# Third and fourth token block share up_w and fc1_w, by seven half-size products; the second block's last product becomes the plain one

## The chip, the cores and the metric

The kernel runs on one core of a Trainium2 chip. Its time is in device microseconds (us); the time before is the median of three runs. A profile is one execution, with the engines named PE (matrix products), PEld (their weight loads), DVE (vector engine), ACT (scalar engine), POOL (GpSimd) and SP (which issues most transfers).

## The reference

One decoder layer over x of 2 x 512 tokens with 1024 features, all f32. What is computed, cut to what matters:

```python
def _L0_attn_ref(x, Wq, bq, Wk, bk, Wv, bv):          # attention inside each token
    q = jnp.einsum('bse,edh->bsdh', x, Wq) + bq         # 32 x 32
    ...                                                 # k, v: 32 x 8, repeated 4 times
    scores = jnp.einsum('bsdh,bseh->bsde', q, k) / np.float32(np.sqrt(D))
    attn = jax.nn.softmax(scores, axis=-1)
    out = jnp.einsum('bsde,bseh->bsdh', attn, v)
def _L0_xattn_ref(x1, x2, ...):                         # per batch
    return jnp.matmul(fake_quant(x1, ...), fake_quant(x2, ...))
def _L0_ffn_ref(hidden_states, gate_w, up_w, down_w, fc1_w, fc2_w, expert_w, ln_gamma, ln_beta):
    logits = jnp.einsum('bsh,he->bse', hidden_states, gate_w)
    routing_weights, selected_experts = jax.lax.top_k(logits, K)
    h = jax.nn.relu(jnp.einsum('bsh,hi->bsi', hidden_states, up_w)) ** 2
    shared_out = jnp.einsum('bsi,ih->bsh', h, down_w)
    x_latent = jnp.einsum('bsh,hl->bsl', hidden_states, fc1_w)
    expert_out = jnp.einsum('bsl,lm->bsm', x_latent, expert_w)
    moe_out = expert_out * jnp.sum(routing_weights, axis=-1, keepdims=True)
    routed_out = jnp.einsum('bsl,lh->bsh', moe_out, fc2_w)
    return _layernorm(shared_out + routed_out, ln_gamma, ln_beta)
x = _layernorm(x + attention(x)); x = _layernorm(x + xattn(x, ctx)); x = _layernorm(x + ffn(x))
```

up_w is 1024 x 2048, down_w 2048 x 1024, fc1_w 1024 x 512, and expert_w x fc2_w (called e2) is 512 x 1024.

## The kernel before

The 1024 tokens are eight tiles of 128, and two tiles make a block of 256; there are four blocks (0 and 1 of batch 0, 2 and 3 of batch 1). Each engine runs its own instructions in the order in which they were laid out, and waits at an instruction whose operand isn't there.

*Front (to 153 us).* `load_xT`, `project_qk` (L148) and `project_v` project all tiles; `fill` lays out side work, the quantised context of batch 0 and e2 (L417). Queries, keys and values of tiles 2 to 7 go to DRAM and are fetched back on POOL's queue.

*Token path.* `token_path` takes the tiles one after another. Attention is on DVE: `scores` (L433, L439), `exponentials`, `attend` (L464, L470, and L485, which adds the result to the row). Then ACT normalises the row aside (`normalise_aside`, with a power on POOL at L323), and `cross` quantises it on ACT (up to L590), transposes it by a DMA on ACT's queue (L593) and multiplies it with the quantised context on PE (py, L607). Another normalisation follows, and `hand_over` transposes the row on PE (L129) into x2T and adds beta to the row by an accumulating DMA from an SBUF tile. `context_beside` makes the context of batch 1 while block 0 and 1 are in work; `context_row` sums its columns on PE (pc, L548).

*Block loop.* For each block, `ffn` does the gate (L708), then 16 products of up_w and 4 of fc1_w (L745: eight matmuls of 128x128 by 128x256 each), with relu (L772) and square (L773) on ACT, and the product with the routing rows on DVE (L786). The weights are loaded by SP, 1 MB for two products, into two buffers (wstream). Each block loads all of them for itself. Between the products the driver at the end of the kernel lets the token path of the next block move on, paced by `PACE`; PE's order is therefore a mix of products, crossings and transposes.

*Down product.* Block 0 uses `down`: 20 units of 128 rows (16 of down_w, 4 of e2), each times two token tiles and two halves of the output (L866, 128x512). Blocks 1 to 3 use `down_seven` (`BY_SEVEN = 1`): a product of 2 x 2 sub-blocks by seven products of half size in place of eight. It needs sums of the units (`unit_sums`, L893 to L896), sums of the weights (`weight_sums`, L906 to L908), both on DVE, seven products (L952, 128x256) in the order 1, 6, 7, 5, 4, 2, 3, and combinations of their results on ACT and DVE (L963 to L972). `finish` normalises, scales and adds the residual row; for blocks 0 to 2 the last normalisation is put aside on ACT (`store_aside`), for block 3 it is done at once at the end.

*Buffers.* Four buffers hold token rows (xpool). PSUM has eight banks: four in ps_dn, two in ps_mm, two in ps_tr.

Of the kernel before, what the change touches and what calls it, by code (L numbers as in the profile page):

```python
# [9 lines left out]
F32 = mybir.dt.float32  # L10
# [17 lines left out]
def kernel(  # L28
# [45 lines left out]
    PACE = (0.9, 0.8, 0.8, 0.8)  # L74
    GW = 32
    NK = NI + NL
    BY_SEVEN = 1
# [7 lines left out]
    xpool = ctx.enter_context(tc.tile_pool(name="xc", bufs=4))  # L85
# [8 lines left out]
    ps_dn = ctx.enter_context(tc.tile_pool(name="ps_dn", bufs=4, space=PSUM))  # L94
    front = ExitStack()
# [5 lines left out]
    identb = const.tile([P, P], BF16, name="identb")  # L101
# [14 lines left out]
    bqk = const.tile([P, 2 * DG], F32, name="bqk")  # L116
    bv_ge = const.tile([P, G, D], F32, name="bv_ge")
# [45 lines left out]
    def new_qkv(t, away):  # L163
        bufs = KEPT if away else 2
        qk = attp.tile([P, 2 * DG], F32, tag="s12" if away else "qk", name=f"qk_{t}", bufs=bufs)
        v = attp.tile([P, G, D], F32, tag="s4" if away else "v", name=f"v_{t}", bufs=bufs)
        return qk, v
# [30 lines left out]
    brow = attp.tile([P, E], F32, tag="s", name="brow", bufs=2)  # L198
    bqk_row = attp.tile([P, E], F32, tag="s", name="bqk_row", bufs=2)
# [6 lines left out]
    ones_row = const.tile([P, P], F32, name="ones_row")  # L206
# [77 lines left out]
    beta = const.tile([P, E], F32, name="beta")  # L284
# [80 lines left out]
    def fill():  # L365
# [3 lines left out]
        for t in range(TB, NT):  # L369
            for _ in range(2):  # L370
                next(aside, None)
            if t == NT - 3:
                nc.sync.dma_start(gamma, ln_gamma.partition_broadcast(P))
                nc.sync.dma_start(beta, ln_beta.partition_broadcast(P))
            ps = projection_psum(t)
            following = None
            for k in range(KE):
                project_qk(ps[0], xT, k)
                project_v(ps[1], xT, k)
                if k == 3:  # L380
                    yield 5.2
                if k == 4 and t + 1 < NT:

                    following = load_xT(t + 1)
                    lay_bias(t + 1)
                    yield 1.3
            xT = following
            projected(t, *ps)
            yield 5.2
# [15 lines left out]
        for l in range(NL):  # L405

            while l >= NL // 2 and 1 not in crossed:
                yield 1.0
            if l == NL // 2:
                with tc.issue_after(expert[0].ins):  # L410
                    held.pop()()
            row = work.tile([P, E], F32, tag="work", name=f"e2_{l}")
            for n in range(2):
                ps = ps_mm.tile([P, HALF], F32, tag="mm", name=f"pe2_{l}_{n}")
                with tc.issue_after(crossed[1].ins) if l >= NL // 2 else ExitStack():
                    for m in range(NL):
                        expert[0] = nc.tensor.matmul(  # L417
                            ps, exT[:, m, ts(l, P)], fc2[m // 2][:, m % 2, ts(n, HALF)],
                            start=(m == 0), stop=(m == NL - 1),
                        )  # L420
                nc.scalar.copy(row[:, ts(n, HALF)], ps)
                yield 3.5
            nc.gpsimd.dma_start(e2[ts(l, P), :], row)


    def scores(t, qk, behind=None):
        q3 = qk[:, 0:DG].rearrange("p (d g) -> p d g", g=G)
        k3 = qk[:, DG : 2 * DG].rearrange("p (e g) -> p e g", g=G)
        s = attp.tile([P, D, D], F32, tag="s", name=f"s_{t}", bufs=2)
        for c in range(D // DC):  # L430
            prod = attp.tile([P, DC * D * G], F32, tag="prod", name=f"pqk_{t}_{c}", bufs=2)
# [22 lines left out]
    def attend(t, xc, s, v):  # L454
# [6 lines left out]
        o = attp.tile([P, D, G], F32, tag="o", name=f"o_{t}")  # L461
        for c in range(D // DC):
            prod = attp.tile([P, DC * D * G], F32, tag="prod", name=f"pav_{t}_{c}", bufs=2)
# [30 lines left out]
    def context_tiles(b):  # L494

        cq = cqs[b] = const.tile([P, KC, E], BF16, tag="cq", name=f"cq_{b}")
# [9 lines left out]
    def context_beside(b):  # L506
# [20 lines left out]
        cq = cqs[b] = const.tile([P, KC, E], BF16, tag="cq", name=f"cq_{b}")  # L527
# [13 lines left out]
    def context_row(b, cq):  # L541
        crow = const.tile([P, E], F32, tag="crow", name=f"crow_{b}")
        for h in range(E // HALF):
            pc = ps_mm.tile([P, HALF], F32, tag="mm", name=f"pc_{b}_{h}")

            with tc.issue_after(projecting[0].ins):
                for k in range(KC):
                    nc.tensor.matmul(  # L548
                        pc, onesb, cq[:, k, ts(h, HALF)], start=(k == 0), stop=(k == KC - 1)
                    )  # L550
# [7 lines left out]
    crossed, held, lately, up_to = {}, [], [None], [0]  # L558
# [6 lines left out]
    def cross(t, xc, cq, crow):  # L565
# [3 lines left out]
        aT = attp.tile([P, KC, P], BF16, tag="aT", name=f"aT_{t}")  # L569
# [29 lines left out]
        for h in range(E // HALF):  # L599

            if t < TB or up_to[0] >= t // TB:
                py = ps_mm.tile([P, HALF], F32, tag="mm", name=f"py_{t}_{h}")
            else:
                py = ps_dn.tile([P, HALF], F32, tag="dn", name=f"py_{t}_{h}")
# [19 lines left out]
    def token_path():  # L624
# [3 lines left out]
        for blk in range(NBLK):  # L628
            xcs = []
            x2T = []  # L630
            for i in range(TB):
# [35 lines left out]
                def hand_over(blk=blk, t=t, i=i, xc=xc, x2T=x2T):  # L667
                    if not x2T:
                        x2T.append(attp.tile([P, KE, NB], F32, tag="x2T", name=f"x2T_{blk}"))
# [3 lines left out]
                    nc.gpsimd.dma_start(xc, beta, accum_op=ALU.add)  # L673
# [3 lines left out]
                if t == 0 or up_to[0] < blk:  # L677
                    held.append(hand_over)
# [20 lines left out]
    def ffn(blk, xcs, xT):  # L699
        (xT,) = xT  # L700
        t0 = blk * TB
        xcs_of[blk] = xcs
# [9 lines left out]
        lg = small.tile([P, NB], F32, tag="lg", name=f"lg_{blk}", bufs=1)  # L712
        nc.scalar.copy(lg, pg[:, :NB])
        yield 1.5


        rwb = pools["ffn"].tile([P, NB], F32, tag="rwb", name=f"rwb_{blk}")

        rwms = []

        def routing():
            for i in range(TB):
                pl = ps_tr.tile([P, NE], F32, tag="tr", name=f"plg_{t0 + i}")
                nc.tensor.matmul(pl, lg[:, ts(i, P)], sel, start=True, stop=True)
                top = small.tile([P, 8], F32, tag="top", name=f"top_{t0 + i}")
                nc.vector.max(top, pl)
                rw = small.tile([P, 1], F32, tag="rw", name=f"rw_{t0 + i}")
                nc.vector.tensor_add(rw, top[:, 0:1], top[:, 1:2])
                rwm = small.tile([P, P], F32, tag="rwm", name=f"rwm_{t0 + i}", bufs=2)
                nc.vector.tensor_copy(rwm, rw.to_broadcast([P, P]))  # L730
                rwms.append(rwm)

        def routing_rows():

            for i, rwm in enumerate(rwms):
                pw = ps_tr.tile([P, P], F32, tag="tr", name=f"pw_{t0 + i}")
                with tc.issue_after(lately[0].ins):
                    nc.tensor.transpose(pw, rwm, ident)
                nc.scalar.copy(rwb[:, ts(i, P)], pw)
# [10 lines left out]

        h, sums = [], []

        def piece(k):
            if k % 4 == 0:
                h.append(pools["h"].tile([P, TB, 4, P], F32, tag="h", name=f"h_{blk}_{k // 4}"))
            return h[-1][:, :, k % 4, :]

        def halves(t):
            return t.rearrange("p (i n) -> p i n", n=P)

        def sums_due():

            while blk >= BY_SEVEN and len(sums) < len(h) - 1:
                sums.append(unit_sums(blk, len(sums), h[len(sums)]))

        for c in range(INT // CW):
# [9 lines left out]
            sums_due()  # L776
            if c == 1:
                routing()
            if c == INT // CW - 2:
                routing_rows()  # L780
        for c in range(LAT // CW):
# [6 lines left out]
            sums_due()  # L788

        up_to[0] = blk + 1  # L790
        if (blk + 2) * TB == S // P:
            later.append(context_beside(1))
        while held:
            held.pop(0)()
        if blk < BY_SEVEN:
            yield from down(blk, h)
        else:
            sums.append(unit_sums(blk, len(sums), h[-1]))
            yield from down_seven(blk, h, sums)
# [16 lines left out]
    def finish(blk, i, y, parts, stats=None):  # L816
# [8 lines left out]
        if blk < NBLK - 1:  # L825
# [6 lines left out]
        nc.vector.scalar_tensor_tensor(y, y, rstd, xcs_of[blk][i], ALU.mult, ALU.add)  # L832

# [21 lines left out]
    def down(blk, h):  # L855
# [4 lines left out]
        for c in range(NK // 2):  # L860
            w = down_rows(f"dn_{blk}_{c}", 2 * c, 2, 0, E)
            for k in range(2):
# [7 lines left out]
                beside(1)  # L870
# [40 lines left out]
    def down_seven(blk, h, units):  # L911
# [17 lines left out]
        while g < len(groups):  # L929
# [27 lines left out]
            yield 6.1 * along  # L957
# [24 lines left out]
    def block_of(step):  # L982
        return step if isinstance(step, tuple) else None

    ready, w_tok, w_fill = None, 0.0, 0.0
    while ready is None:
        step = next(tokens)
        ready = block_of(step)
        w_tok += 0.0 if ready else step
# [15 lines left out]
    for blk in range(NBLK):  # L1005
        now, ready = ready, None
        w_tok = w_ffn = 0.0
        for weight in ffn(*now):
            w_ffn += weight
            while blk + 1 < NBLK and ready is None and w_tok * PACE[blk] < w_ffn:  # L1010
                step = next(tokens)
                ready = block_of(step)
                w_tok += 0.0 if ready else step
        while blk + 1 < NBLK and ready is None:
            ready = block_of(next(tokens))
# [33 lines left out]
```

## Time and profile before

| | us |
|---|---|
| median of three runs (733.94 to 737.42) | 736.36 |
| profiled execution | 740.23 |
| its span | 738.5 |
| PE starts block 0, 1, 2, 3 (gate) | 152.69, 302.62, 451.75, 592.40 |
| PE ends the last product | 724.92 |
| L745, all up_w and fc1_w products, PE busy | 226.4 + 55.9 |
| L866, plain down of block 0 | 69.2 |
| L952, down by sevens of blocks 1, 2, 3, four groups | 61.0 + 61.0 + 60.9 + 30.5 |

| stretch, us | PE busy | DVE busy | ACT busy | granted clock |
|---|---|---|---|---|
| 153 to 303 | 148.70 | 143.50 | 54.54 | 1.00 |
| 303 to 450 | 143.69 | 132.51 | 60.00 | 0.99 |
| 450 to 592 | 141.60 | 70.86 | 44.34 | 1.00 |
| 592 to 740 | 132.07 | 56.38 | 22.39 | 0.96 |

A line of the groups reads: line, engine, operation, output<-inputs, shapes, count, busy time, mean ns of one, and the idle time just before them with what ended it. The granted clock is the share of full speed that the throttle left to PE. Matmuls overlap, so that the mean ns of one is longer than the distance from one to the next.

### The profile page before, as it was taken

Reading aid. Unit: us, or ns where it says so; the run is one execution under the profiler, and the core shown is the slowest. Engines: PE = TensorE matmul, PEld = TensorE weight load, DVE = VectorE, ACT = ScalarE, POOL = GpSimd, SP = SyncE. Lnnn points to the kernel's source line nnn. Section 1 sums busy time; section 2 is a strip of 40 time slices with the busy share of each in tenths; the row PEclk is TensorE's granted clock in tenths of the full one; section 3 lists DMA queues with packets and bytes.
Section 4 is the critical chain, followed back from the end, with each engine's and each line's share of the span. In section 5 each row is a group of like instructions: output and inputs, shape, how many; then the busy total and the mean of one; then the engine's idle time right before and its main releaser. Section 6 shows DMA issues by size and latency. Waiting matters only on the chain. (4 is left out here: it accounts for less than half of the span.)

```text
span 738.5 us, 7687 instructions
## 1 busy us (share of the span) xinstructions
PE 708.4 (96%) x3002; PEld 533.7 (72%) x3012; DVE 523.5 (71%) x573; ACT 248.7 (34%) x433; POOL 69.2 (9%) x96
## 2 busy tenths in 40 slices
PE   6999998999999999998999999999999999999992
PEld 3665653468876444686788788887887888888882
DVE  4789986699989999999999968913246371013636
ACT  2087633222573205377560021374401013400001
POOL 2001221100001002130010011010000010100001
PEclk9999998999999999999999999999999999999997
DMA  8999635294546547764456446564654645635401
GB/s 280 343 272 366 185 68 167 71 306 132 181 129 190 163 175 241 217 218 143 129 142 193 165 164 181 195 204 144 168 173 168 199 119 167 217 126 170 171 1 57
DMA packets 84660, 131.09 MB, mean 178 GB/s; under 512 B 10816, under 2 KB 55360, under 8 KB 84624
## 3 DMA queue, kind: packets, MB, share of 16 engines
q1 hardware_dynamic: 70448, 109.85, 44.8%
q0 software_dynamic: 6496, 18.39, 9.8%
q10 hardware_dynamic: 7680, 2.36, 1.5%
q8 instruction: 24, 0.39, 0.2%
q14 instruction: 12, 0.10, 0.0%
HBM read 113.55 MB, written 11.01 MB: 169 GB/s over the span
## 5 line engine op out<-in xcount | busy, mean ns | idle before, releaser
L745 PE MATMUL pu<-x2T,up 128*128 128x256 f32 x1024 | 226.4, 382 | 4.6 <-ACT relu L772 2.6
L745 PEld LDWEIGHTS pu<-x2T,up 128*128 128x128 f32 x1024 | 194.5, 191 | 34.1 <-ACT relu L772 3.0
L906 DVE TENSOR_TENSOR tt<-dn 128x1024 f32<-128x1024 f32 x30 | 36.6, 1222 | 57.9 <-DMA dn<-in_L_ffn_down_w_dram 37.8
L439 DVE TENSOR_REDUCE s<-pqk 128x256 f32<-128x2048 f32 x32 | 72.4, 2277 | 0.1
L433 DVE TENSOR_TENSOR pqk<-qk 128x2048 f32<-128x2048 f32 x32 | 72.4, 2282 | 0.0
L464 DVE TENSOR_TENSOR pav<-s,v 128x2048 f32<-128x2048 f32 x32 | 72.3, 2277 | 0.0
L470 DVE TENSOR_REDUCE o<-pav 128x64 f32<-128x2048 f32 x32 | 72.1, 2269 | 0.0
L866 PE MATMUL pd<-dn,h 128*128 128x512 f32 x160 | 69.2, 592 | 0.0
L148 PE MATMUL pqk<-wqkv,xT 128*128 128x512 f32 x128 | 65.8, 615 | 1.5 <-DVE wqkv L229 1.2
L772 ACT ACTIVATE relu<-pu 128x256 f32<-128x256 f32 x64 | 24.2, 379 | 112.2 <-PE pu L745 112.2
L952 PE MATMUL ps<-tt,h 128*128 128x256 f32 x240 | 61.0, 379 | 0.5 <-DVE y L967 0.5
L952 PE MATMUL ps<-dn,s 128*128 128x256 f32 x240 | 61.0, 379 | 0.1
L952 PE MATMUL ps<-dn,h 128*128 128x256 f32 x240 | 60.9, 379 | 0.0
L866 PEld LDWEIGHTS pd<-dn,h 128*128 128x128 f32 x160 | 30.2, 190 | 37.0 <-issue 36.8
L745 PE MATMUL pl<-x2T,fc 128*128 128x256 f32 x256 | 55.9, 379 | 0.0
L745 PEld LDWEIGHTS pl<-x2T,fc 128*128 128x128 f32 x256 | 48.6, 190 | 6.7
L893 DVE TENSOR_TENSOR s<-h 128x256 f32<-128x256 f32 x15 | 6.3, 422 | 63.6 <-ACT h L773 63.5
L952 PEld LDWEIGHTS ps<-tt,h 128*128 128x128 f32 x240 | 45.5, 190 | 7.0 <-DVE y L967 0.9
L952 PEld LDWEIGHTS ps<-dn,s 128*128 128x128 f32 x240 | 45.5, 190 | 6.7 <-DVE dn L907 0.5
L952 PEld LDWEIGHTS ps<-dn,h 128*128 128x128 f32 x240 | 45.3, 190 | 6.2
L323 POOL TENSOR_TENSOR rstd<-ve,neg_half 128x1 f32<-128x1 f32 x20 | 20.9, 1044 | 257.2 <-ACT ve L321 257.2
L963 ACT COPY y<-ps 128x256 f32<-128x256 f32 x6 | 2.2, 372 | 125.3 <-PE ps L952 125.3
(161 smaller groups left out, 796.9 us busy)
## 6 DMA issues: line engine op xcount, KB each, us to landing
dn<-in_L_ffn_down_w_dram SPq DMA_DIRECT2D x32, 1024.0 KB, 5.1
up<-in_L_ffn_up_w_dram SPq DMA_DIRECT2D x32, 1024.0 KB, 5.3
fc<-in_L_ffn_fc_w_dram SPq DMA_DIRECT2D x10, 1024.0 KB, 5.5
dn<-e SPq DMA_DIRECT2D x8, 1024.0 KB, 5.0
xs<-in_x_dram SPq DMA_DIRECT2D x8, 512.0 KB, 7.8
wq<-in_L_attn_Wq_dram SPq DMA_DIRECT2D x8, 512.0 KB, 6.3
xc<-in_x_dram SPq DMA_DIRECT2D x8, 512.0 KB, 5.5
ctx<-in_ctx_dram SPq DMA_DIRECT2D x8, 512.0 KB, 6.9
```

The lines of the kernel that those rows point to most:

```text
L148: projecting[0] = nc.tensor.matmul(pqk, xT[:, k, :], wqkv[k][:, 0 : 2 * DG], start=(k == 0), stop=(k == KE - 1))
L323: nc.gpsimd.tensor_tensor(rstd, ve, neg_half, ALU.pow)
L433: nc.vector.tensor_tensor(prod.rearrange("p (d e g) -> p d e g", d=DC, g=G), q3[:, ts(c, DC), :].unsqueeze(2).to_broadcast([P, DC, D, G]), ...
L439: nc.vector.tensor_reduce(s[:, ts(c, DC), :].rearrange("p d e -> p (d e)"), prod.rearrange("p (c g) -> p c g", g=G), AX.X, ALU.add,)
L464: nc.vector.tensor_tensor(prod.rearrange("p (d g e) -> p d g e", d=DC, g=G), s[:, ts(c, DC), :].unsqueeze(2).to_broadcast([P, DC, G, D]), ...
L470: nc.vector.tensor_reduce(o[:, ts(c, DC), :].rearrange("p d g -> p (d g)"), prod.rearrange("p (c e) -> p c e", e=D), AX.X, ALU.add,)
L745: lately[0] = nc.tensor.matmul(ps[:, :NB], ws[:, k, wcols], xT[:, k, :], start=(k == 0), stop=(k == KE - 1))
L772: nc.scalar.activation(r, ps, AF.Relu)
L866: lately[0] = nc.tensor.matmul(pd[i][n], h[kk // 4][:, i, kk % 4, :], w[:, k, ts(n, HALF)], start=(kk == 0), stop=(kk == NK - 1),)
L893: nc.vector.tensor_tensor(s1, a21, a22, ALU.add)
L906: nc.vector.tensor_tensor(tt[:, 0:2], w[:, 1], w[:, :, 0], ALU.subtract)
L952: began[m] = lately[0] = nc.tensor.matmul(banks[m], units[jj][m][:, k, :], weights[gg][m][:, k, :], start=begins and not second, stop=(jj ...
```

## The change

Blocks 2 and 3 are taken together in a new function `ffn_pair`, which meets up_w and fc1_w once. It sees the two blocks' transposed rows as a matrix of 2 x 2 (halves of the 1024 features by block) and 256 weight columns as 2 x 2 (halves of the features by 128 columns). Each of ten steps loads 1 MB of weights, makes four weight sums on DVE, and does seven products of four matmuls (128x128 by 128x256) in the order 1, 2, 3, 5, 6, 7, 4; six DVE instructions and an ACT copy combine them into both blocks' results. Four sums of the rows are made once at the start. Even steps use the four banks of ps_dn, odd ones those of ps_mm and ps_tr. Then `down_seven` runs for block 2 and for block 3, with block 3's unit sums laid out in block 2's second half. Blocks 0 and 1 both use the plain `down`.

All tokens go through attention and crossing before the pair. The driver has one pace (0.64) and lets the token path run on through both blocks, so the context row of batch 1 and the crossings of tiles 4 to 7 stand in blocks 0 and 1. Crossing and context row take a bank of ps_dn while a block is in its up products, of ps_mm otherwise. Transposes of block 3's tiles wait for the pair.

Token rows get six buffers instead of four, beta is read from DRAM by the accumulating DMA, what only the token path needs is moved to a pool that is closed before the pair (`tokp`), and a pool `late` takes its place. Block 2's `finish` normalises on DVE at once. The gate and routing of a block become a generator, `gate_of`.

```diff
-    PACE = (0.9, 0.8, 0.8, 0.8)
+    PACE = 0.64
-    BY_SEVEN = 1
+    PAIR = NBLK - 2
...
-    xpool = ctx.enter_context(tc.tile_pool(name="xc", bufs=4))
+    xpool = ctx.enter_context(tc.tile_pool(name="xc", bufs=6))
...
+    tokens_only = ExitStack()
+    tokp = tokens_only.enter_context(tc.tile_pool(name="tok", bufs=1, side="right"))
...
+    def spare_bank(name):
+        if phase[0] == "up":
+            return ps_dn.tile([P, HALF], F32, tag="dn", name=name)
+        return ps_mm.tile([P, HALF], F32, tag="mm", name=name)
...
-                    nc.gpsimd.dma_start(xc, beta, accum_op=ALU.add)
-                if t == 0 or up_to[0] < blk:
-                    held.append(hand_over)
+                    nc.gpsimd.dma_start(xc, ln_beta.partition_broadcast(P), accum_op=ALU.add)
+                if t == 0 or up_to[0] < blk or blk > PAIR:
+                    held.append((blk, hand_over))
...
+    UP_ORDER = (1, 2, 3, 5, 6, 7, 4)
+
+    def ffn_pair(xcs_a, xa, xcs_b, xb):
...
+        def prepare():
+            g = len(steps)
+            if g == NK // 2:
+                return
+            src, c = (up3, g) if g < NI // 2 else (fc13, g - NI // 2)
+            w = wstream.tile([P, KE, CW], F32, tag="wa", name=f"pair_{g}")
+            nc.sync.dma_start(w, src[:, :, ts(c, CW)])
+            a11, a12, a21, a22 = (
+                w[:, ts(half, KH), ts(u, P)] for u in range(2) for half in range(2)
+            )
+            ss = pools["sums"].tile([P, 3, KH, P], F32, tag="tt", name=f"ss_{g}")
+            s1, s2, s4 = ss[:, 0], ss[:, 1], ss[:, 2]
+            nc.vector.tensor_tensor(s1, a21, a22, ALU.add)
+            nc.vector.tensor_tensor(s2, s1, a11, ALU.subtract)
+            nc.vector.tensor_tensor(a21, a11, a21, ALU.subtract)
+            nc.vector.tensor_tensor(s4, a12, s2, ALU.subtract)
+            steps.append({1: a11, 2: a12, 3: s4, 4: a22, 5: s1, 6: s2, 7: a21})
+        prepare()
+        prepare()
+        routings = [gate_of(blk, x) for blk, x in zip(blks, xs)]
...
+        nc.vector.tensor_tensor(t1, b12, b11, ALU.subtract)
+        nc.vector.tensor_tensor(t3, b22, b12, ALU.subtract)
+        nc.vector.tensor_tensor(t2, b22, t1, ALU.subtract)
+        nc.vector.tensor_tensor(t4, b21, t2, ALU.subtract)
+        moving = {1: b11, 2: b21, 3: b22, 4: t4, 5: t1, 6: t2, 7: t3}
...
+        for g in range(NK // 2):
...
+            for m in UP_ORDER:
+                for k in range(KH):
+                    with tc.issue_after(lately[0].ins):
+                        lately[0] = nc.tensor.matmul(
+                            banks[m], steps[g][m][:, k, :], moving[m][:, k, :],
...
+            nc.scalar.copy(c11, banks[1])
+            nc.vector.tensor_tensor(c12, banks[6], c11, ALU.add)
+            nc.vector.tensor_tensor(c21, banks[7], c12, ALU.add)
+            nc.vector.tensor_tensor(c22, banks[5], c21, ALU.add)
+            nc.vector.tensor_tensor(c12, banks[5], c12, ALU.add)
+            nc.vector.tensor_tensor(c21, banks[4], c21, ALU.add)
+            nc.vector.tensor_tensor(cs[:, 0], b[1], cs[:, 0], ALU.add)
+            if g < NI // 2:
+                nc.scalar.activation(cs, cs, AF.Relu)
...
+                    acted[0] = nc.scalar.activation(to, units, AF.Square)
...
+                    nc.vector.tensor_tensor(to, units, rows, ALU.mult)
+            beside(3)
+            prepare()
...
+        down_seven(PAIR, h[0], sums, next_block)
+        down_seven(PAIR + 1, h[1], next_sums)
...
-        if blk < NBLK - 1:
+        if blk < PAIR:
...
+        if blk < NBLK - 1:
+            normalise(y, f"3_{blk}_{i}")
+            nc.gpsimd.dma_start(rows, y)
+            return
...
-                beside(1)
+                beside(2)
...
+    for blk in range(PAIR):
+        while len(ready) <= blk:
+            w_tok += advance()
+        for weight in ffn(*ready[blk]):
+            w_ffn += weight
+            while alive and w_tok * PACE < w_ffn:
+                step = advance()
+                alive = step is not None
+                w_tok += step or 0.0
+    while alive:
+        alive = advance() is not None
+    let_in()
+    tokens_only.close()
...
+    ffn_pair(*ready[PAIR][1:], *ready[PAIR + 1][1:])
```

## The prediction

> **What bounds the kernel now.** I read the page's busy row and slices first, then its costliest groups, then PE's timeline by block, then who is behind PE's idle times.
>
> ```profile
> span 738.5 us, 7687 instructions
> PE 708.4 (96%) x3002; PEld 533.7 (72%) x3012; DVE 523.5 (71%) x573; ACT 248.7 (34%) x433; POOL 69.2 (9%) x96
> PE   6999998999999999998999999999999999999992
> DVE  4789986699989999999999968913246371013636
> ...
> L745 PE MATMUL pu<-x2T,up 128*128 128x256 f32 x1024 | 226.4, 382 | 4.6 <-ACT relu L772 2.6
> ```
>
> PE works in every slice but the ends, so the kernel is as long as PE's list of matmuls and the gaps in it. DVE is full only while tokens go through attention (to about 440 us) and half idle afterwards. The chain of waits covers just the tail of 13 us. So two questions decide: how many matmul records go, and which waits appear in PE's order. The page counts an f32 matmul as two records (4 blocks x 16 products x 8 matmuls = 512, shown as 1024), and its 382 ns overlap. What PE pays is the spacing in a burst without gaps:
>
> ```profile
> 214.84 13.98 PE L745 MATMUL pl<-x2T,fc 128*128 128x256 f32 x64
> ...
> 281.05 13.90 PE L866 MATMUL pd<-dn,h 128*128 128x512 f32 x32
> ```
>
> The columns are start, length, line, count. Less the last record's overhang (0.16), 64 records of 128x256 take 13.82: 0.2159 us each, so a product of eight matmuls is 3.455. A 128x512 record takes 0.4294.
>
> **Fewer and more matmuls.** Up_w and fc1_w for blocks 2 and 3: 2 x 20 products x 3.455 = 138.2 before; 10 steps x 28 matmuls x 2 records x 0.2159 = 120.9 after: -17.3. Block 1's down product: 280 records x 0.2159 = 60.4 by sevens before; 160 x 0.4294 = 68.7 plain after: +8.3. Sum -9.0.
>
> **Moved.** The context row of batch 1, four crossings (3.4 us each on PE), transposes (0.9 a tile) and the gates are the same instructions elsewhere: zero on PE. Beta's accumulation from DRAM, in place of SBUF, lands (6.1 us before) tens of us ahead of the finish that reads it: zero. The pair's sums cost DVE, per step of 12.09 us of PE:
>
> ```profile
> L908 DVE TENSOR_TENSOR tt<-dn 128x512 f32<-128x512 f32 x30 | 20.4, 683 | 0.5
> ...
> L967 DVE TENSOR_TENSOR y<-ps,y 128x256 f32<-128x256 f32 x6 | 2.5, 412 | 0.0
> ...
> up<-in_L_ffn_up_w_dram SPq DMA_DIRECT2D x32, 1024.0 KB, 5.3
> ```
>
> Four sums of 128x512 are 2.7 us, five combinations of 128x256 and one of 128x512 another 2.8, and every second step 1.7 of unit sums: some 6.4 of 12.09, on an engine without tokens by then. ACT gets a copy, a relu and two squares, about 3 us. The load of step g+2 starts when step g has left its buffer; 5.3 to land plus 2.7 of sums is 8.0, inside the step between, with 4 to spare. Cost zero; that cover is the third case below.
>
> **Waits that go.** Idle times in PE's order that belong to code rearranged: 0.47 before a product at 204 us, 0.49 and 0.85 at 418 and 643, and this one:
>
> ```profile
> 328.30 3.41 POOL L323 TENSOR_TENSOR rstd<-ve,neg_half 128x1 f32<-128x1 f32 x1 [1.25 <-ACT ve L321]
> ...
> 331.74 0.29 ACT L327 ACTIVATE shift<-rstd,parts 128x1 f32<-128x1 f32 x1 [2.55 <-POOL rstd L323]
> ...
> 334.53 12.31 PE L745 MATMUL pu<-x2T,up 128*128 128x256 f32 x48 [2.56 <-ACT relu L772]
> ...
> 335.00:338.00 3.00, 3.00 (x10) 2.36 (x9) 2.28 (x6) 2.94 (x5) 0.09 (x1) 0.59 0.99 365
> ```
>
> Read it downwards: the power on POOL (0.56 median) took 3.41, ACT waited with block 0's rows, its relus came late, PE stood 2.56. The last row is a window: the granted clock (0.59) is its third number from the end; 48 records took 12.15 to the next start, not 10.36: 1.8 lost. Sum 0.47 + 0.49 + 0.85 + 2.56 + 1.8 = 6.2.
>
> [...]
>
> **Waits that come.** Order by order I set PE's arrival against the operand. A token's chain, from attention's last DVE step to the transposed operand of its crossing:
>
> ```profile
> 188.82 1.21 DVE L485 SCALAR_TENSOR_TENSOR xc<-xc,o 128x1024 f32<-128x1024 f32 x1
> ```
> ```profile
> 233.72 1.21 DVE L485 SCALAR_TENSOR_TENSOR xc<-xc,o 128x1024 f32<-128x1024 f32 x1
> ```
> ```profile
> 244.11 1.25 ACTq L593 DMA_TRANSPOSE aT<-a  x1
> ```
>
> Tile 3: 233.72 to 244.11, plus 3.2 to landing = 247.3, so 13.6 us. DVE is full with the same work, so tile 2's operand comes at 188.8 + 13.6 = 202.4.
> - Its crossing stands after the 13th up product, not the 16th: PE came there at 211.60, less 3 x 3.455 and 0.9 of routing rows now behind it: 200.3. Wait 2.1 (0 to 5).
> - Tile 3's crossing is in time (PE 248.6, operand 247.3). Its transposes come 11 plain matmuls later (9.4), PE 261.2; ACT has tile 4's exponential and a context load's issue ahead, then the aside normalisation (parts to xc took 5.0 at 194.1): about 262.9. Wait 1.8 (0 to 5).
> - Tile 4's crossing has 2 us in hand, 6 has 8, 7 has 13. Tile 5's finds ACT on block 0's two rows: 1.2 (0 to 4).
> - One fc1 product behind an h product on DVE, queued behind a reduction (2.28): 0.7. One up load behind tile 6's input load on SP, which waits for a buffer that tile 0's finish frees: 0.7. Block 3's gate behind ACT's copies: 0.4. (Each 0 to 2.)
> - Block 2 to block 3: the down products now follow each other. DVE has block 2's finish (per tile two L820 at 0.74, one 1.28, two stats at 0.69, a scaling at 0.81, two powers to wait for) between block 3's weight sums. Adding up DVE's order from the boundary, groups 1 and 2 are ready 0.5 before PE, group 3 at 19.5 against 18.1. Wait 1.5 (0 to 5).
> - Clock after the 2 us idles: half of the 1.8 above, 1.0 (0 to 4).
>
> Sum 9.4. Nothing is lower than zero here, since a wait can't be negative.
>
> [...]
>
> Net: -9.0 - 6.2 + 9.4 = -5.8; span 732.7. Tail unchanged. The profiled run was 740.23 (1.73 outside its span), 3.87 over the median; scaled, 736.36 x 732.7 / 738.5 = 730.6, and I say 730.
>
> **Rivals.**
> - *The new waits hardly come* (the arrivals were set pessimistically). Span 738.5 - 9.0 - 6.2 = 723.3, plus 2 for what is left of them: 725.3, median 723. For: every wait is under 2.2 us and rests on arrivals good to 2. Against: DVE is full (9s to slice 23), so tokens can't be early.
> - *Tokens late.* All eight now have to cross before the pair, and DVE does 44 us a tile; two of the four tight places (tiles 2, 3, 4, 5) meet a long power (3.41 for 0.55) and lose clock: 2 x (2.9 + 1.8) less the 1.0 counted: span 732.7 + 8.4 = 741.1, median 739, no change. For: POOL's long powers fell in this stretch, beside full DVE. Against: 0.56 median of 20.
> - *Loads set the pair's step* (slower). Only two buffers hold the 1 MB steps, and the load starts after a buffer is left. From 9.4 us of landing on (12.09 - 2.7) each of eight steps waits. At 11 us: 8 x 1.6 = 12.8 and up to 0.9 of clock each: span 745 to 753, median 743 to 750. For: the longest up load took 8.6. Against: the median 5.3, with context and token loads beside it that the pair doesn't have.
> - The matmuls not falling as said: excluded by the order of instructions, 280 in the pair.
>
> **Chances.** Forecast (725 to 735) 0.55; waits hardly come 0.15; tokens late 0.17; loads 0.13. Range 720 to 742: it takes in the first three and touches the last. 0.5% is 3.7 us, what a measurement can tell: faster is below 732.7, slower over 740.0. Faster: 0.55 x 0.85 + 0.15 + 0.02 = 0.64. Slower: 0.13 + 0.05 + 0.01 = 0.19. Same: 0.17.
>
> **What would show it.** The pair's line on PE with 560 records and steps of 12.1 us; block 1's down at 0.43 a record; PE's idles at tile 2's and 5's crossings, tile 3's transposes, and some 18 us into block 3's down; windows with low clock behind them; pair loads near 5.3. It is wrong if pair steps are longer than 12.5, if a pow on POOL of 3 us stands before a PE idle, or if PE reaches the pair later than DVE's last token step by much more than 13 us.

## The result, and the profile after

| | kernel before | changed kernel |
|---|---|---|
| median of 20 runs each, us | 736.89 (733.94 to 740.46) | 735.25 (733.81 to 737.86) |
| ratio, 95% interval | | 0.9979 (0.9965 to 0.9993) |
| span of the profiled execution, us | 738.5 | 731.8 |

The change gains 0.21%, 1.6 us; forecast were 6. Its time lies inside the range that was given (720 to 742), the size of the gain does not fit. The two profiled spans differ by 6.7 us, much as forecast, but the first of them belongs to a long execution (740.23, near the longest of its 20 runs, 740.46) and the second to the shortest of its own (733.81). The span alone would have confirmed the sum by accident.

The page of the changed kernel, its busy row and slices, then two groups:

```profile
span 731.8 us, 7278 instructions
PE 696.0 (95%) x2803; PEld 493.8 (67%) x2812; DVE 545.1 (74%) x619; ACT 240.0 (33%) x389; POOL 64.0 (9%) x96
PE   6999999999799899999899999999999999999992
DVE  4799986899989779999899950455454663779736
...
L982 PE MATMUL pd<-dn,h 128*128 128x512 f32 x320 | 138.8, 592 | 0.0
L768 PE MATMUL pu<-x2T,up 128*128 128x256 f32 x512 | 112.7, 380 | 1.1 <-DMA up<-in_L_ffn_up_w_dram 1.1
```

The work is what the diff says: up products of two blocks in place of four, plain down products of two blocks in place of one. New are the 7 and the 8s in PE's slices 11, 14 and 20. Who is behind them stands in the waits of PE, summed by releaser (total, times, longest):

```profile
PE py L611 <- DMA aT<-a: 9.8, 3, 4.0
...
PE pu L768 <- DMA up<-in_L_ffn_up_w_dram: 1.1, 1, 1.1
PE pt_x L133 <- ACT x2T L134: 0.9, 1, 0.9
...
PE pt_x L133 <- ACT xc L331: 0.3, 1, 0.3
```

Three crossings stand 9.8 us waiting for their transposed operand. In the kernel before that line was 0.3 us. PE's timeline has the places:

```profile
200.83 3.40 PE L611 MATMUL py<-cq,aT 128*128 128x512 bf16 x15 [4.00 <-DMA aT<-a]
...
249.46 5.31 PE L611 MATMUL py<-cq,aT 128*128 128x512 bf16 x15 [2.79 <-DMA aT<-a]
...
357.18 3.63 PE L611 MATMUL py<-cq,aT 128*128 128x512 bf16 x15 [2.99 <-DMA aT<-a]
```

These are tiles 2, 3 and 5. The second took 5.31 where the others took 3.40 and 3.63: the clock fell behind that wait (granted 0.72 from 249 to 255 us). The pair itself runs as worked out. Its first matmul and the first of block 2's down product:

```profile
474.87 0.92 PE L869 MATMUL pp<-x2T,pair 128*128 128x256 f32 x3
```
```profile
597.27 1.03 PE L1068 MATMUL ps<-dn,h 128*128 128x256 f32 x4
```

122.4 us for 120.9 of products and the routing between them, with no idle time; the two down products follow at full pace to PE's end at 718.3.

### The profile page after: what moved, and what is told of

Same layout as the page of the kernel before. It is cut to its first block, busy times and chain, and to the rows that moved or that the text cites. A ratio compares the mean times of both kernels' runs of the same rounds, so it can differ in the third digit from the quotient of the medians.

```text
span 731.8 us, 7278 instructions
## 1 busy us (share of the span) xinstructions
PE 696.0 (95%) x2803; PEld 493.8 (67%) x2812; DVE 545.1 (74%) x619; ACT 240.0 (33%) x389; POOL 64.0 (9%) x96
## 5 line engine op out<-in xcount | busy, mean ns | idle before, releaser
L982 PE MATMUL pd<-dn,h 128*128 128x512 f32 x320 | 138.8, 592 | 0.0
L768 PE MATMUL pu<-x2T,up 128*128 128x256 f32 x512 | 112.7, 380 | 1.1 <-DMA up<-in_L_ffn_up_w_dram 1.1
L982 PEld LDWEIGHTS pd<-dn,h 128*128 128x128 f32 x320 | 60.5, 190 | 72.9 <-issue 72.2
L768 PEld LDWEIGHTS pu<-x2T,up 128*128 128x128 f32 x512 | 96.6, 190 | 15.7 <-ACT relu L786 1.8
L157 PEld LDWEIGHTS pv<-wqkv,xT 128*128 128x128 f32 x128 | 24.3, 190 | 24.2 <-issue 22.0
L1068 PE MATMUL ps<-dn,h 128*128 128x256 f32 x160 | 40.4, 379 | 0.0
L1068 PE MATMUL ps<-tt,h 128*128 128x256 f32 x160 | 40.4, 379 | 0.0
L1068 PE MATMUL ps<-dn,s 128*128 128x256 f32 x160 | 40.4, 379 | 0.0
L611 PE MATMUL py<-cq,aT 128*128 128x512 bf16 x121 | 29.9, 395 | 10.2 <-DMA aT<-a 9.8
L157 PE MATMUL pv<-wqkv,xT 128*128 128x256 f32 x128 | 35.6, 379 | 0.0
```

Source lines behind the costliest of these rows:

```text
L157: nc.tensor.matmul(pv[:, :DG], xT[:, k, :], wqkv[k][:, 2 * DG : 3 * DG], start=(k == 0), stop=(k == KE - 1),)
L611: crossed[t] = nc.tensor.matmul(py, aT[:, k, :], cq[:, k, ts(h, HALF)], start=(k == 0), stop=(k == KC - 1))
L768: lately[0] = nc.tensor.matmul(ps[:, :NB], ws[:, k, wcols], xT[:, k, :], start=(k == 0), stop=(k == KE - 1))
L982: lately[0] = nc.tensor.matmul(pd[i][n], h[kk // 4][:, i, kk % 4, :], w[:, k, ts(n, HALF)], start=(kk == 0), stop=(kk == NK - 1),)
L1068: began[m] = lately[0] = nc.tensor.matmul(banks[m], units[jj][m][:, k, :], weights[gg][m][:, k, :], start=begins and not second, stop=(jj ...
```

## The experiments

Ratios are to the kernel before on the same chip, and a ratio can differ by 0.1% from the quotient of two medians. The median of the kernel before was 736.77 beside before_again, after_again, late_crossings and pair_undone; 738.81 beside before_plain1, b1_seven, crossings_later and ready_operand; 739.02 beside after_third, crossings_later_2, later_a and later_b; 736.96 beside pe_transposes and later_b_2.

**Was the profiled execution of before a fair one? (before_again: no edit)**

> The kernel before, unchanged, profiled once more. Theory: the execution profiled before the prediction was an unlucky one. Its 2.50 us wait at 114 us, the 3.41 us power on POOL with the 2.56 us wait at 334 us, and the 3.7 us of slow clock behind the two are not in every execution; without them the span is near 735 and block 0 starts near 149 instead of 152.7. Rival: they belong to the kernel, the span is again near 738 and both waits are there.

One run, 736.73, span 734.9. Its waits of PE:

```profile
PE pu L745 <- ACT relu L772: 2.4, 1, 2.4
...
PE pu L745 <- DMA up<-in_L_ffn_up_w_dram: 1.1, 1, 1.1
PE pe L417 <- DVE xc L611: 1.1, 1, 1.1
PE pu L745 <- ACT rwb L739: 0.9, 1, 0.9
```

Half and half. The wait in the front was 1.1 instead of 2.50, without a slow clock (the two records behind it took 1.13 for 2.08), and block 0 began at 148.75 instead of 152.69: that varies from one execution to the next (2.2 in that of before_plain1 below). The wait for the relu, with a power of 3.41 us ahead of it and the slow clock behind it (48 records again in 12.31 us, granted 0.72 from 331 to 337 us), is there again at 330.9: it belongs to the kernel.

**The changed kernel again (after_again, after_third: no edit)**

> The changed kernel, unchanged. Ratio to the kernel before 0.998 (0.9965 to 0.9993 as measured). The theory expects the same waits in front of the crossings of tiles 2, 3 and 5 (4.0, 2.8 and 3.0 us in the first profile), within a microsecond or two, since the token path on the vector engine is full there. The rival (they are an accident of one execution, by slow landings of the transposes) expects at most one of them over 2 us.

> The changed kernel, unchanged, so that it stands on the same chip as the next three. Ratio to the kernel before 0.997 to 0.998; waits before the crossings of tiles 2, 3 and 5 as in its two earlier profiles (4.0 to 4.3, 2.8 to 2.9, 3.0).

Ratios 0.9974 (0.9955 to 0.9993) and 0.9956 (0.9939 to 0.9972), spans 732.7 and 734.8. The three waits came again: 4.25, 2.84, 2.96 and 4.16, 2.82, 3.14. They belong to the kernel, as the theory said.

**Is the pair worth its matmuls? (pair_undone)**

```diff
-    ffn_pair(*ready[PAIR][1:], *ready[PAIR + 1][1:])
+    for blk in (PAIR, PAIR + 1):
+        for _ in ffn(*ready[blk]):
+            pass
```

(`ffn` gets the unit sums and uses `down_seven` for blocks 2 and 3.)

> The changed kernel, but blocks 2 and 3 meet up_w and fc1_w one after the other with the plain products (2 x 20 of eight matmuls) as before; all else as changed, the token path included. Theory: the pair is worth what its matmuls are, 80 records of 0.2159 us = 17.3 us, so 17 us slower than the changed kernel, ratio to the kernel before 1.021. Rival (the pair's steps lose time to their sums, loads and combinations): clearly less than 17 us, say 10 or less, ratio 1.011 or lower.

752.82 against 734.85 for after_again on the same chip: 18.0 us slower, spans 750.6 and 732.7; ratio to before 1.0236 (1.0212 to 1.0259). The pair gives all of its 17.3, and its sums, loads and combinations cost PE nothing.

**What does the plain down product of block 1 cost? (before_plain1, b1_seven)**

In the kernel before, one line:

```diff
-    BY_SEVEN = 1
+    BY_SEVEN = 2
```

> The kernel before with one edit of the change alone: block 1's down product is the plain one. Theory: 8.3 us more on PE, less the 0.5 us wait on a combination at 418 us and whatever the freed vector engine brings: ratio to the kernel before 1.010 to 1.011. Rival (the plain one frees the vector engine so much that waits go): under 4 us slower, ratio below 1.005.

742.12, ratio 1.0048 (1.0031 to 1.0066), 3.5 us: less than half of 8.3. The theory's 1.010 is excluded; the rival's bound of 1.005 lies inside the interval. Block 1 took 152.7 us from gate to gate against 148.3 in before_again. POOL's power ahead of the relus, and PE's wait that follows from it:

```profile
326.29 1.82 POOL L323 TENSOR_TENSOR rstd<-ve,neg_half 128x1 f32<-128x1 f32 x1 [1.25 <-ACT ve L321]
```
```profile
330.93 0.48 PE L745 MATMUL pu<-x2T,up 128*128 128x256 f32 x1 [0.65 <-ACT relu L772]
```

PE passes this place at 330.93, in before_again at 330.90, although block 0 began 1.6 us later here (150.31): the wait took up the difference, 0.65 of its 2.4 is left, and the 48 records behind it took 10.63 us, without a slow clock (granted 1.00 from 320 to 340 us). The power is 1.6 us shorter than the 3.41 of before_again and ends at 328.1 in both, 0.4 after a product on DVE that ends at 327.7 in both. So a part of the 4.2 us booked under "waits that go" is had by the plain product alone, without the pair. How much of that is owed to DVE's missing sums and how much to the late front, one profile doesn't tell.

In the changed kernel the other way round:

```diff
-        yield from down(blk, h)
+        if blk == 0:
+            yield from down(blk, h)
+        else:
+            sums.append(unit_sums(blk, len(sums), h[-1]))
+            yield from down_seven(blk, h, sums)
```

(The unit sums are laid out between block 1's products, and `down_seven` lets the token path move on.)

> The changed kernel with block 1's down product by sevens again. On PE 8.3 us less; on the vector engine some 35 us more (ten groups of 2.6, unit sums of 8.5) in block 1's second half, where it had 35 us of idle time in the changed kernel's trace, 27 of them while waiting for tile 7's crossing and the block's end. Theory (the vector engine has that room, only the crossing order matters): 5 to 8 us below the changed kernel, ratio to the kernel before 0.987 to 0.991. Rival (the tokens come late for it, as the change's author of the order would fear): no gain or slower, ratio 0.998 or more, with a wait before tile 7's crossing or its transposes.

742.96, ratio 1.0055 (1.0037 to 1.0073): the rival is right. PE before tile 7's crossing and before its transposes:

```profile
471.96 5.67 PE L611 MATMUL py<-cq,aT 128*128 128x512 bf16 x15 [6.87 <-DMA aT<-a]
...
482.89 1.54 PE L133 MATMUL pt_x<-ident,xc 128*128 128x128 f32 x8 [4.25 <-ACT xc L331]
```

The room on DVE that the expectation counted lies behind the last token; the sums come before it, and the last tile is late by more than the 8.3 us saved.

**Can the crossings be met later? (late_crossings, crossings_later, crossings_later_2)**

The first try lets the whole token path in later:

```diff
-    PACE = 0.64
+    PACE = 0.62
-    w_tok, w_ffn, alive = 0.0, 0.0, True
+    w_tok, w_ffn, alive = 20.0, 0.0, True
```

> The changed kernel with the token path let in later on PE: pace 0.62 in place of 0.64, and a lead of 20 for the products. No work is added or taken away; the crossings of tiles 2, 3 and 5 move 5 to 7 us back in PE's order. Theory (the change's gain was given back in waits before these crossings): the three waits of 9.8 us and 1.9 us of slow clock behind them go, span 11 us shorter, ratio to the kernel before 0.983. Rival (vector engine is the bound of blocks 0 and 1, so that PE waits at the next place instead): within 2 us of the changed kernel, ratio 0.998, with waits before the crossings of tiles 6 and 7 or the transposes at the pair's start.

739.4, ratio 1.0039 (1.0021 to 1.0056): slower, and neither theory had it. Three lines, the scalar engine's issue of tile 2's transpose, then PE:

```profile
201.76 1.25 ACTq L601 DMA_TRANSPOSE aT<-a  x1
```
```profile
208.27 5.98 PE L611 MATMUL py<-cq,aT 128*128 128x512 bf16 x15 [3.92 <-DMA aT<-a]
...
318.57 1.94 PE L719 MATMUL pg<-x2T,gate 128*32 128x256 f32 x16 [5.11 <-DVE ve_f L299]
```

The transpose was issued at 196.31 in after_again. ACT runs the token's steps between the relus of the products, so the operand moved back with the crossing, and the tokens' DVE work got in the way of block 0's finish.

The second try moves the crossing alone, by a longer step behind the transpose and a shorter one behind the tile:

```diff
+    GAP = {2: 27, 3: 28, 4: 20, 5: 28}
+    TAIL = {2: -9, 3: -10, 4: -2, 5: -10}
...
-            yield 12.0
+            yield GAP.get(t, 12.0)
...
-            yield 6.0
+            yield TAIL.get(t, 6.0)
```

> The changed kernel; only the crossings of tiles 2, 3, 4 and 5 stand later in PE's order (by one, two, one and three products or their like in down matmuls: 3.5, 6.9, 3.4 and 10.3 us), while the scalar engine's steps that make their operands stay where they were, unlike in the run with the later pace. Theory (the operand's chain is late and PE only has to meet it later): the waits of 4.0, 2.8 and 3.0 us and 1.9 us of slow clock go to under 2 us together, span 8 to 10 us below the changed kernel, ratio to the kernel before 0.985 to 0.988. Rival (the vector engine stands behind the crossing in its own order, so a later crossing makes the next tile's operand later by the same): less than 4 us gained, ratio 0.992 or more, and waits at the next crossings or at the pair's start.

> The kernel with the crossings of tiles 2 to 5 later, again. Its span lay 3.7 us below the changed kernel's, its ratio 0.0107 (7.9 us) below, each taken on another chip. Theory (waits taken away minus new ones: 10.1 of waits and 1.7 of clock, against 2.2, 2.3, 1.0 and 0.6): 4 to 8 us below the changed kernel on the same chip. Rival (the difference was the chip's): less than 2.

Ratios 0.9867 (0.9839 to 0.9894) and 0.9882 (0.9858 to 0.9905). On the chip that ran the changed kernel too, 729.57 against 735.57: 6.0 us less. The spans, 729.0 and 728.7, lie 3.7 below after_again's and 6.1 below after_third's: less than the 8 to 10 of the first expectation, within the 4 to 8 of the second. The waits of tiles 3 and 5 are gone, tile 2 still waits 2.2 and 1.5, and block 1's gate waits 2.3 and 2.9 for a bank that tile 4's crossing has left to DVE.

**What do the waits for operands cost in all? (ready_operand)**

```diff
-                        py, aT[:, k, :], cq[:, k, ts(h, HALF)], start=(k == 0), stop=(k == KC - 1)
+                        py, aT[:, k, :] if t < TB else cq[:, k, 0:P], cq[:, k, ts(h, HALF)],
+                        start=(k == 0), stop=(k == KC - 1)
```

> The changed kernel, but the crossings of tiles 2 to 7 multiply a block of the quantised context in place of the row's transposed codes, so that no crossing waits for its operand (the transposes are still made; the output is not the reference's). Theory: all that the waits for operands cost goes: 9.8 us of waits and 1.9 us of clock, span 11 to 13 us below the changed kernel, ratio to the kernel before 0.981 to 0.984. Rival (the vector engine, full in blocks 0 and 1, holds PE up elsewhere): less than 6 us below.

725.24, ratio 0.9819 (0.9794 to 0.9843), which is 1.4 to 1.6% under the changed kernel's ratios, some 10 to 12 us; span 723.7, 9.0 under after_again. The ratio is the theory's, the span fell short of its 11 to 13; fc1 products now wait 2.0 in all for DVE. What the change lacks, and more, stands in these waits.

**Why is the operand late? (pe_transposes)**

```diff
-            nc.scalar.dma_start_transpose(aT, a)
-            yield 12.0
+            if t == 0:
+                nc.scalar.dma_start_transpose(aT, a)
+                yield 12.0
+            else:
+                yield 8.5
+                pt = ps_tr.tile([P, KC, P], BF16, tag="tr", name=f"pta_{t}")
+                with behind_products():
+                    for k in range(KC):
+                        nc.tensor.transpose(pt[:, k, :], a[:, ts(k, P)], identb)
+                nc.scalar.copy(aT, pt)
+                yield 3.5
```

> The changed kernel, but tiles 2 to 7 are transposed by PE (eight transposes and a copy on the scalar engine) and not by a transfer; their crossings stand where they were or a product later. Theory (the operand is late because the transposing transfer lands in 3.8 to 6.2 us where a weight load or a reload of queries runs beside it, against 3.1 alone): PE gets some 3.7 us more work (six tiles at 0.6), and the waits for operands shrink from 10 us to under 4 in all, so 3 to 6 us below the changed kernel, ratio to the kernel before 0.989 to 0.994. Rival (the operand is late because of what goes before the transpose, on the vector and the scalar engine): waits of 8 us or more in all, before the transposes now, and 2 to 4 us slower than the changed kernel, ratio 1.000 to 1.003.

728.4, ratio 0.9873 (0.9853 to 0.9892), span 724.7: 8.0 under after_again, though PE has 48 transposes more. The ratio is 0.8 to 1.1% under the changed kernel's, 6 to 8 us. Of the waits for the crossings' operands one is left in PE's list:

```profile
PE pta L609 <- ACT a L598: 1.3, 1, 1.3
```

The three crossings start at 199.59, 245.56 and 350.27, earlier than the 200.83, 249.46 and 357.18 of the changed kernel, so it isn't that PE meets them later. Without the transfer the waits go but for 1.3 us, which is somewhat more than the 3 to 6 us of the theory. Two things this run doesn't separate: the transfer's usual 3.1 us go along with what it takes beside a load, and tile 3's codes are ready earlier too, since tile 2's crossing is no longer late (below).

**A version that beats both (later_a, later_b, later_b_2)**

Both start from crossings_later. later_a has GAP {2: 31, 3: 28, 4: 12, 5: 24}; later_b has 18 for tile 4 (TAIL makes up for it: the two still add up to 18) and

```diff
-        pg = ps_mm.tile([P, HALF], F32, tag="mm", name=f"pg_{blk}")
+        bank, tag = (ps_tr, "tr") if blk == 1 else (ps_mm, "mm")
+        pg = bank.tile([P, HALF], F32, tag=tag, name=f"pg_{blk}")
```

> As before, with tile 2's crossing one more product later, tile 5's earlier by 3.4 us and tile 4's where the changed kernel has it. Theory: the 2.2 us wait at tile 2's crossing goes, and the 2.3 us wait of block 1's gate (its bank is still read by the vector engine's step behind tile 4's crossing) becomes shorter, unless tile 4's operand isn't there: 2 to 4 us below the run before this one. Rival (the vector engine's order sets both): within 1 us of it.

> As the run before, but tile 4's crossing stays 3.4 us later, and block 1's gate takes a bank of the transposes' pool, not the one that tile 4's crossing uses. Theory: the gate's wait of 2.3 us shrinks to under 1: 2 to 4 us below the kernel with later crossings. Rival (the first product takes the same bank and waits in its place): the wait moves to the product, nothing gained.

> The kernel with later crossings and the gate's other bank, again, on another chip. Theory: ratio to the kernel before 0.983 to 0.988, waits of PE for crossings and gate under 2 us in all. Rival (its first median was a lucky draw of six runs): ratio 0.990 or more.

later_a 726.9, ratio 0.9848 (0.9818 to 0.9879); later_b 726.91, 0.9865 (0.983 to 0.9899), and on another chip 725.63, 0.9853 (0.9826 to 0.9879). The changed kernel beside the first two ran 735.57, so both gain 8.7 us on it (8.0 and 6.7 by the ratios). Both lie 2.7 us under crossings_later_2, as expected, with intervals that overlap its own. In later_a no crossing waits, but an up load came 2.6 us late at 326; in later_b the gate's wait became 0.9 before the first product, in the bank that the rival named: the wait moved, and most of it went. The intervals don't tell the two apart.

## Why the prediction was wrong, step by step

From before_again (734.9) to after_again (732.7), both without the long wait in the front, the span changes by -2.2:

| term | forecast | found | where from |
|---|---|---|---|
| fewer and more matmuls | -9.0 | -9.0 | pair 122.4 us without idle time, pair_undone +18.0; plain down 69.4 us a block (L982), 69.2 before |
| waits and clock that go | -6.2 | -6.9 | 2.43 + 1.8, 0.88, 0.50, 0.49, 0.29, and 0.5 less before an up load |
| crossings of tiles 2, 3, 5 | +3.3 | +10.3 | 4.25, 2.84 + 0.22, 2.96 |
| slow clock behind them | +1.0 | +2.6 | 1.1 and 1.5: tile 2's crossing took 4.54 for 3.40, tile 3's 5.09 for 3.62 |
| transposes of tile 3 | +1.8 | +0.2 | 0.15 |
| fc1 product, up load, gate of block 3 | +1.8 | +0.9 | 0.94 before block 2's transposes |
| block 2 to block 3 | +1.5 | 0 | no idle time there |
| sum | -5.8 | -1.9 | measured -2.2 |

The two lines on the crossings came out 8.6 us higher than forecast, the three below them 4.0 lower, which by luck hid half of it.

**The matmuls and the waits that go were right**, to 0.7 us, though before_plain1 has a part of the waits go without the pair.

**The step that failed is "plus 3.2 to landing = 247.3, so 13.6 us": one chain for tiles 2 and 3.** Counted from the start of DVE's last attention step to the landing of the transpose, the chain took 16.7 us in tile 2 (183.85 to 200.56) and 16.6 in tile 3 (232.80 to 249.41). Both were 3 us longer than the sum had, for different reasons.

*Tile 3: the landing.* From DVE's step to the issue it took 10.4, as worked out; 3.2 to landing was the median of seven transposes, and here it was 6.2. The issues of SP, POOL and ACT near tile 3's transpose in the changed kernel, with KB and us to landing, then the same near tile 4's:

```profile
dn<-in_L_ffn_down_w_dram SPq DMA_DIRECT2D x1, 1024.0 KB, 5.2
qk<-qkv_d POOLq DMA_DIRECT2D x1, 256.0 KB, 4.5
aT<-a ACTq DMA_TRANSPOSE x1, 6.2
```
```profile
qk<-qkv_d POOLq DMA_DIRECT2D x1, 256.0 KB, 3.6
aT<-a ACTq DMA_TRANSPOSE x1, 3.1
```

Issued together with a weight load it lands in 6.2 (tile 5: 5.7); tile 4's, with the last such load issued 4.4 us earlier, in 3.1. The 16 traces agree: the 29 transposes with a weight load issued less than 1 us before or after them took 5.4 to 8.7, the 42 with none from 4 us before to 1 us after 3.0 to 3.2; the 35 others took 3.1 to 6.9. No run moved a load by itself, so that the load is the cause is read from these places alone. The trace of before shows it already for the same tile:

```profile
dn<-in_L_ffn_down_w_dram SPq DMA_DIRECT2D x1, 1024.0 KB, 5.2
qk<-qkv_d POOLq DMA_DIRECT2D x1, 256.0 KB, 3.6
aT<-a ACTq DMA_TRANSPOSE x1, 5.6
```

It cost nothing there: it had landed by 249.7, and the crossing stood at 277.59. "Tile 3's crossing is in time (PE 248.6, operand 247.3)" becomes operand 249.46, PE 246.67: 2.8 of wait and 1.7 of clock where the sum had none. Of the 4.1 us from 1.3 in hand to 2.8 late, 3.0 are the landing. The rest is that PE came 1.9 earlier than worked out and DVE's step only 0.9. For tile 5 the landing was longer by 2.5 than 3.2 and the wait went from 1.2 to 3.0.

*Tile 2: a long power on POOL (wait 2.1 forecast, 4.0 found).* Its chain took 12.9 to the issue where tile 3's takes 10.4. The power on POOL and the step of ACT that waits for it:

```profile
187.19 2.72 POOL L326 TENSOR_TENSOR rstd<-ve,neg_half 128x1 f32<-128x1 f32 x1 [11.53 <-ACT ve L324]
```
```profile
189.94 0.29 ACT L330 ACTIVATE shift<-rstd,parts 128x1 f32<-128x1 f32 x1 [2.60 <-POOL rstd L326]
```

In tile 3's chain this power took 0.64, so 2.1 of the 2.5 us are its length. It is not an accident: it took 2.72 or 2.73 in all three executions of the changed kernel, and 0.59 to 1.00 at tile 2 in the two of before. The landing adds 0.6 (3.8 for 3.2). PE came 3.5 us earlier than worked out and DVE's step 5.0, most of both because block 0 began at 148.66 and not at 152.69. No run took the power away, so its share of the wait is worked out and not shown.

**A late crossing also holds DVE**, which the forecast priced at nothing. DVE's lines behind tile 2's crossing in the changed kernel:

```profile
202.54 0.75 DVE L615 SCALAR_TENSOR_TENSOR xc<-py,ns,xc 128x512 f32<-128x512 f32 x1 [1.12 <-PE py L611]
204.27 0.75 DVE L615 SCALAR_TENSOR_TENSOR xc<-py,ns,xc 128x512 f32<-128x512 f32 x1 [0.97 <-PE py L611]
207.61 1.22 DVE L458 TENSOR_REDUCE den<-s 128x32 f32<-128x1024 f32 x1 [1.45 <-ACT s L454]
```

3.5 us idle on the engine that sets the tokens' pace, of which 0.97 stands in pe_transposes too, and tile 3's transpose is issued at 244.15 in after_again against 240.59 in before_again, 3.6 later. In pe_transposes, where tile 2's crossing isn't late, tile 3's codes are ready at 239.3, against 243.2 in the changed kernel. By these numbers the wait at tile 2 also makes tile 3's operand late, and either these 3.9 us or the 3.0 of the landing would cover tile 3's wait of 2.8.

**The rivals.** "Tokens late" had the right places (tiles 2, 3 and 5 among its four), and its 739 lies nearer to 735.25 than the forecast's 730. Its agent, a long power on POOL, was there at one of them, tile 2, the longest wait; at tiles 3 and 5 the powers took 0.64 and 0.56, and the transfers were what took longer. "Loads set the pair's step" is refuted: the pair's loads of up_w landed in 5.3, the median of before.

## What to carry to other kernels

When a change moves a wait onto the path, take the duration of each link of that very chain from the trace, at its place and with what runs beside it, not the median of its group or the chain of a neighbour. Profile a kernel twice before a wait of 2 us is booked as its property: of two such waits here one came back whole, the other was 1.1. And when products are saved on the engine that bounds, ask which operands of others it will now meet too early: here a move of a few crossings by a few us brought 6 to 9 us, where the change as it stood brought 1.6.

## What the runs showed of the hardware

- In these traces an idle time had no fixed price in clock. The same three waits, 9.8 to 10.1 us in all, lost clock in different places: after tile 2's wait the first profile had none, and after_third ran its crossing in 5.74 us. Of the nine waits of the three executions five lost 1.1 to 2.3 us, and four none (4.00, 2.99, 2.96 and 2.82). Windows from 201 to 207 us of the first profile and of after_third (length, busy times, then granted clock, third from the end):

```profile
201.00:207.00 6.00, 6.00 (x29) 4.06 (x28) 3.08 (x6) 1.91 (x5) 0.00 (x0) 1.00 0.01 3
```
```profile
201.00:207.00 6.00, 5.75 (x16) 2.34 (x16) 1.44 (x3) 0.00 (x0) 0.00 (x0) 0.58 0.01 3
```

  Idle before it: 4.00 and 4.16. The spans of the three profiles, 731.8, 732.7 and 734.8, rise with the losses, 1.7, 2.6 and 4.0 us. The length of an idle time doesn't order the losses: those of 2.43 (before_again), 2.56 (before), 2.79 and 2.84 us (the first two profiles of the changed kernel) lost 1.5 to 1.8 us, the one of 4.00 none. What decides it is not shown.
- The power on POOL of one number per row had a median of 0.56 us over the 20 at L323 in the trace of before. One of them took 3.41 in both executions of before, at the same place; in the changed kernel the one at tile 2 took 2.72. In before_again it runs from 324.68, beside DVE's product of 128x2048 (325.37 to 327.65), and ends 0.4 after it; in before_plain1 one of 1.82 ends 0.4 after such a product, and in the changed kernel the one of 2.72 (187.19 to 189.91) does so too (product 187.20 to 189.48). No run moved such a product away, so that it is what makes the power long is not shown.
